# Attention and ternary feed-forward on one core: input rows of the second batch entry fetched and normalised one step earlier, in five buffers instead of three, and two start-up transposes in other PSUM buffers

## The chip, the core and the metric

The kernel runs on one core of a Trainium2 chip. The metric is device time in microseconds (us), the median of several runs. The profile is one execution of its own, with a time of its own. Engines are named as the profile names them: PE (matmul), PEld (its weight loads), DVE, ACT, POOL, and SP, whose queue issues the DMAs.

## The reference, cut to what matters

All data are fp32. Two batch entries of 1024 tokens and 512 features go through attention with 16 heads of 128 and then through a feed-forward layer whose three weights are rounded to -1, 0 or 1 times a scale.

```python
def attn(x):                                   # x: (2, 1024, 512)
    q, k, v = (einsum('bsd,hed->bhse', x, W) for W in (W_Q, W_K, W_V))
    scores = einsum('bhse,bhme->bhsm', q, k) / sqrt(128)
    scores = where(causal, -1e9, scores)
    z = einsum('bhsm,bhme->bhse', softmax(scores), v)
    return einsum('bhse,hde->bsd', z, W_O)

def ffn(x):                                    # hidden size 1365
    g = silu(x @ ternary(w1).T) * (x @ ternary(w3).T)
    return g @ ternary(w2).T

x = x + layernorm(attn(layernorm(x)))
out = x + layernorm(ffn(layernorm(x)))
```

## The kernel before

**Tiling.** A batch entry is 8 row tiles of 128 tokens. A head is worked in 8 steps, one for each row tile of queries; tile i needs scores against (i+1) x 128 keys. Two entries of 16 heads give 32 heads of 8 steps, and the loop at L813 to L894 walks them: head n is head n % 16 of entry n // 16. Every projection is done as three products of rounded parts, so weights and inputs are each held in three forms, "lead" (`a`), "low" (`l`) and "difference" (`d`).

**What one step does.** `scores` (L551) multiplies on PE into a PSUM tile `s_ps`, then DVE applies the mask (L561) and takes the row maximum (L565), ACT takes the exponential (L572), DVE the reciprocal of the row sums (L577), and ACT scales the row (L578) into `p_sb`. DVE turns the row in 32x32 squares (L604), SP writes it to DRAM (`hop`, L615) and reads it back turned (`pt`, L631), and PE multiplies it with v (L650). In between, PE does the projections of the next head (q and k: L471 and L478; v: L499) and the output product of a pair of heads (L519, added into `acc` by DVE at L530 and L533). Weights come in by L423; their lead form is made by ACT (L439), their low form by POOL (L440), their difference form by DVE (L446).

**Input blocks.** The rows x of an entry are normalised (L388 on ACT, or L123 on DVE), transposed by PE in four pieces into one PSUM tile (L403, `block_unit`), and read from there into the three forms `xb`: lead on ACT (L407), low on DVE (L408), difference on POOL, in two start-up tiles on DVE (L409). For the first entry this happens at the start, from `acc`. For the second entry row tile t is transposed at step 117 + t, counted over all heads, so in heads 14 and 15: `block_load` (L380) fetches the rows into a buffer `xt` of the pool "x", `normal_unit` normalises them there. The same pool serves the row sums of the feed-forward weights (L148 and L154, heads 0 to 9), the input statistics of the second entry (L354 and L109) and the residual rows (L279).

**Order.** `side[...]` is a list of units of work per step; the units are recorded behind named marks of the step. A scheduler then puts the instructions of each engine into one fixed order, which it chooses by its own estimate of when operands are there and buffers are free. Each engine runs its list strictly in that order, and so does the SP queue; an instruction that waits holds up all behind it on its engine. A tile of a pool gets a buffer that is free or is the first to come free. Pool "ps_m" holds four PSUM buffers (tag `mm`: projections, transposes, products with v), pool "ps_s" two larger ones (scores, and the transposes of the first entry).

**The start.** PE first runs 20 transposes of the identity (`busy(20)`, L703), then the transposes of row tiles 0 and 1, `busy(8)`, those of tiles 2 and 3, `busy(3)`, and then the q and k projections of head 0.

```python
side[block_at - 3 + t].append(lambda t=t: block_load(1, t))     # L752, block_at = 117
side[block_at - 2 + t].append(lambda t=t: normal_unit(1, t))    # L753
```

Of the kernel before, what the change touches and what calls it, by code (L numbers as in the profile page):

```python
# [35 lines left out]
def sandwich_kernel(  # L36
# [85 lines left out]
    def normalise(dst, src, mv, r, t):  # L122
        return nc.vector.tensor_scalar(  # L123
            dst, src, mv[:, t, 0:1], r[:, t : t + 1], ALU.subtract, ALU.mult
        )
# [212 lines left out]
    with ExitStack() as att:  # L338
# [4 lines left out]
        vpool = att.enter_context(tc.tile_pool(name="v", bufs=2))  # L343
        zpool = att.enter_context(tc.tile_pool(name="z", bufs=ZB))
        qpool = att.enter_context(tc.tile_pool(name="q", bufs=2))
        xpool = att.enter_context(tc.tile_pool(name="x", bufs=3))
        ps_s = att.enter_context(tc.tile_pool(name="ps_s", bufs=2, space=PSUM))


# [7 lines left out]
        def stats_units(t):  # L357
            held = {}

            def load():  # L360
                held["x"] = stats_load(1, t)

            return load, lambda: row_stats(mv_in[1][:, t, :], held["x"])
# [14 lines left out]
        def block_load(b, t):  # L378
            normal[b, t] = xt = xpool.tile([P, D], FP, name="xt")
            nc.sync.dma_start(xt, x[b, ts(t, P), :])  # L380

        def normal_unit(b, t):
            if b == 0:
                normal[b, t] = acc[:, t, :]
            xt = normal[b, t]
            if b == 0 and t % 2 == 1:
                return normalise(xt, xt, mv_in[b], r_in[b], t)
            return nc.scalar.activation(  # L388
                xt, xt, AF.Identity, scale=r_in[b][:, t : t + 1],
                bias=shifts[b][:, t : t + 1],  # L390
            )

        def block_unit(b, t):
            k, tl = divmod(t, QT)
            if tl == 0:
                xs[b, k] = [xblocks.tile([P, NC, TB], FR, name="xb") for _ in range(3)]
            xt = normal[b, t]
            if b == 0:
                ps = ps_s.tile([P, NC, P], FP, name="tr", tag="s_ps")
            else:  # L400
                ps = ps_m.tile([P, NC, P], FP, name="tr", tag="mm")
            for c in range(NC):
                newest[0] = nc.tensor.transpose(ps[:, c, :], xt[:, ts(c, P)], ident)  # L403
            lead, low, diff = (form[:, :, ts(tl, P)] for form in xs[b, k])
            eng = nc.vector if b == 0 and tl >= QT // 2 else nc.gpsimd
            return (
                nc.scalar.mul(lead, ps, LEAD / T12),  # L407
                nc.vector.scalar_tensor_tensor(low, lead, -T12, ps, ALU.mult, ALU.add),  # L408
                eng.tensor_tensor(diff, lead, low, ALU.subtract),  # L409
            )  # L410
# [19 lines left out]
        def lead_and_low(kind, n, part, first=False):  # L430

            if (kind, n) not in weights:
                weights[kind, n] = [form(kind, "a"), form(kind, "l")]
            lead, low = (w[:, part] for w in weights[kind, n][:2])
            raw = wraw[kind, n][:, part]
            if first:
                nc.vector.tensor_scalar(lead, raw, LEAD, None, ALU.mult)
            else:
                nc.scalar.mul(lead, raw, LEAD)  # L439
            nc.gpsimd.tensor_tensor(low, raw, lead, ALU.subtract)  # L440
# [241 lines left out]
        @contextmanager  # L682
        def past(*instructions):
            with ExitStack() as order:
                for i in instructions:
                    order.enter_context(tc.issue_after(i.ins))
                yield
# [10 lines left out]
        def busy(times):  # L698
            with ExitStack() as order:
                if newest[0] is not None:  # L700
                    order.enter_context(past(newest[0]))
                for _ in range(times):
                    newest[0] = nc.tensor.transpose(idle, ident, ident)  # L703
# [4 lines left out]
        with past(*done):  # L708
            for kind in range(2):
                lead_and_low(kind, 0, EVERY, first=True)  # L710
            blocks = []
            for t in range(QT):
                blocks.append(block_unit(0, t))
                if t % 2 == 1:
                    busy((8, 3)[t // 2])
        lead, low, diff = blocks[-1]
        with past(diff):
            for kind in range(2):
# [12 lines left out]
        side = [[] for _ in range(N * NT)]  # L731
        at = 0

        def two_steps_each(pairs, at):
            for first, then in pairs:
                side[at].append(first)
                side[at + 2].append(then)
                at += 2
            return at

        for k in range(3):
            pairs, total, last = mean_abs_units(k, xpool)
            at = two_steps_each(pairs, at)
            side[at + 1].append(total)
            side[at + 3].append(last)
        at = two_steps_each([stats_units(t) for t in range(NT)], at)
        side[at + 1].append(lambda: std_unit(1, 0, NT))

        block_at = 2 * (NP - 1) * NT + 5
        assert at + 1 < block_at - 3  # L750
        for t in range(NT):
            side[block_at - 3 + t].append(lambda t=t: block_load(1, t))  # L752
            side[block_at - 2 + t].append(lambda t=t: normal_unit(1, t))  # L753
        at += (1 - at) % 4 + 4
        for stages in ternary_steps(qpool):
            for later, stage in zip((0, 2, 3, 4), stages):
# [46 lines left out]
        for t in range(QT, NT):  # L803
            block_unit(0, t)
# [8 lines left out]
        for n in range(N):  # L813
            g, j = divmod(n, 2)
            b, pr = divmod(g, NP)
# [23 lines left out]
            for t in range(NT):  # L839
                if divmod(block_at + t, NT)[0] == n:  # L840
                    put([(block_at + t) % NT], [lambda t=t: block_unit(1, t)])
# [5 lines left out]
            for i in range(NT):  # L847
# [23 lines left out]
                with behind("max", "half", "exp", of=idx + 1):  # L871
# [4 lines left out]
                    at = g + 1 - j  # L876
# [26 lines left out]
    with ExitStack() as ffn:  # L903
# [4 lines left out]
        xpool = ffn.enter_context(tc.tile_pool(name="xf", bufs=3))  # L908
# [208 lines left out]
```

## Time and profile before

| | us |
|---|---|
| median of 3 runs | 1512.0 |
| the runs | 1510.33 to 1512.47 |
| time of the profiled execution | 1511.27 |
| its span, first to last instruction | 1509.5 |
| PE busy | 1475.6 |
| DVE busy | 1080.6 |
| ACT busy | 792.7 |
| POOL busy | 404.3 |
| mean granted TensorE clock | 0.997 |

Some 1.8 us of the profiled execution's time lie outside its span. All times below are in us from the start of the span. A group "x4" in a timeline is four instructions of one line that follow each other; "[1.27 <-ACT xt L388]" behind a row says that the engine sat idle for 1.27 us before it, until that instruction had ended. SPq rows are the issue of a DMA, not its transfer. Matmuls are pipelined: a row's duration holds the end of its own result, and the next one starts before that.

### The profile page before, as it was taken

To read this page: it belongs to the slowest core of one execution; us is meant where nothing else is said; L and a number is where in the kernel's file an instruction comes from. 1 tells how busy PE (TensorE), PEld (TensorE's weight loads), DVE (VectorE), ACT (ScalarE), POOL (GpSimd) and SP (SyncE) were. 2 spreads that over 40 slices of the span, in tenths; PEclk is the share of its full clock that TensorE was granted. 3 is DMA by queue.
4 is the path that set the end of the run, shared out by engine and by line. 5 is a ranking of instruction groups with operands and counts; after the bars stand their busy time and mean duration, and the time that the engine had idled before them with its cause. 6 is when DMAs were issued, how large, how long until landed. Compare 5 with 4: busy or idle time off the path is not lost.

```text
span 1509.5 us, 21335 instructions
## 1 busy us (share of the span) xinstructions
PE 1475.6 (98%) x7061; PEld 1184.9 (78%) x7061; DVE 1080.6 (72%) x2123; ACT 792.7 (53%) x1566; POOL 404.3 (27%) x472
## 2 busy tenths in 40 slices
PE   8999999999999999999999999999999999999997
PEld 6778888887878787777778787878787877888885
DVE  7767686878786878787777777777777776664444
ACT  4656555555555555666664555555555464444332
POOL 3222222222223333434433333333322110210010
PEclk9999999999999999999999999999999999999999
DMA  3666767676666675758866666666665677530200
GB/s 123 194 194 186 195 184 200 185 202 184 201 191 172 181 206 183 205 166 249 238 200 190 195 192 196 195 195 189 179 179 166 181 216 228 176 102 19 91 28 29
DMA packets 179894, 263.57 MB, mean 175 GB/s; under 512 B 19188, under 2 KB 120564, under 8 KB 175688
## 3 DMA queue, kind: packets, MB, share of 16 engines
q1 hardware_dynamic: 179784, 262.20, 59.5%
q8 instruction: 57, 0.93, 0.3%
q14 instruction: 53, 0.43, 0.1%
HBM read 160.43 MB, written 101.71 MB: 174 GB/s over the span
## 4 chain that ended last, share of the span: by engine, by line
PE 66%; issue 10%; DVE 9%; DMA 7%; ACT 5%; POOL 2%; SPq 1%; DVEq 0%; POOLq 0%; ACTq 0%
PE mm L650 11%; PE mm L471 10%; PE mm L318 10%; PE s_ps L556 10%; PE mm L499 8%; PE mm L519 6%; PE yp L933 5%; PE mm L478 5%; DVE nm L565 3%; DMA hop<-blocks 2%; ACT p_sb L572 2%; DMA wqk<-wk 2%; ACT p_sb L578 1%; POOL kl L440 1%; DVE blocks L604 1%
## 5 line engine op out<-in xcount | busy, mean ns | idle before, releaser
L572 ACT ACTIVATE p_sb<-s_ps,nm 128x128 f32<-128x128 f32 (+7 forms) x256 | 190.0, 742 | 367.3 <-DVE nm L565 360.8
L556 PE MATMUL s_ps<-k,q 128*128 128x512 f32 (+3 forms) x768 | 289.7, 486 | 0.7 <-ACT p_sb L572 0.7
L650 PE MATMUL mm<-pt,v_sb 128*128 128x256 f32 (+1 forms) x1280 | 271.7, 359 | 11.3 <-ACT q L454 3.7
L650 PEld LDWEIGHTS mm<-pt,v_sb 128*128 128x128 f32 x1280 | 238.1, 190 | 48.8 <-ACT q L454 6.2
L578 ACT ACTIVATE p_sb<-p_sb,ri 128x128 f32<-128x128 f32 (+7 forms) x256 | 197.7, 773 | 33.0 <-DVE ri L577 30.5
L565 DVE TENSOR_REDUCE nm<-s_ps 128x1 f32<-128x128 f32 (+7 forms) x256 | 193.7, 757 | 7.1
L604 DVE STREAM_TRANSPOSE blocks<-p_sb 128x128 f32<-128x128 f32 (+7 forms) x256 | 197.1, 770 | 1.2 <-ACT p_sb L578 0.9
L556 PEld LDWEIGHTS s_ps<-k,q 128*128 128x128 f32 x768 | 132.3, 190 | 69.4 <-issue 61.4
L670 POOL TENSOR_TENSOR zd<-za,zl 128x256 fp32r<-128x256 f32 x128 | 94.7, 739 | 328.0 <-DVE zl L667 319.7
L561 DVE TENSOR_TENSOR s_ps<-s_ps,causal 128x128 f32<-128x128 f32 x256 | 75.4, 295 | 136.1 <-PE s_ps L556 135.6
L499 PE MATMUL mm<-va,xb 128*128 128x256 f32 x512 | 158.5, 310 | 0.0
L499 PE MATMUL mm<-vd,xb 128*128 128x256 f32 x512 | 144.9, 283 | 0.9 <-POOL xb L409 0.9
L499 PE MATMUL mm<-vl,xb 128*128 128x256 f32 x512 | 144.6, 282 | 0.0
L471 PE MATMUL mm<-xb,qa 128*128 128x512 f32 x256 | 119.6, 467 | 1.0 <-ACT xb L407 1.0
L471 PE MATMUL mm<-xb,ka 128*128 128x512 f32 x256 | 112.3, 439 | 0.0
L499 PEld LDWEIGHTS mm<-vl,xb 128*128 128x128 f32 x512 | 97.7, 191 | 7.1 <-issue 4.1
L499 PEld LDWEIGHTS mm<-va,xb 128*128 128x128 f32 x512 | 97.7, 191 | 7.1 <-issue 3.9
L471 PE MATMUL mm<-xb,ql 128*128 128x512 f32 x256 | 101.7, 397 | 0.0
L471 PE MATMUL mm<-xb,kl 128*128 128x512 f32 x256 | 100.7, 393 | 0.1
L499 PEld LDWEIGHTS mm<-vd,xb 128*128 128x128 f32 x512 | 97.7, 191 | 1.1 <-POOL xb L409 1.1
L601 POOL MEMSET blocks<- 128x128 f32 x128 | 26.2, 205 | 263.1 <-DMA hop<-blocks 185.2
L533 DVE TENSOR_TENSOR acc<-acc,mm 128x512 f32<-128x512 f32 x128 | 86.1, 683 | 12.7 <-ACT acc L528 5.4
(162 smaller groups left out, 2777.3 us busy)
## 6 DMA issues: line engine op xcount, KB each, us to landing
hop<-blocks SPq DMA_DIRECT2D x32, 1024.0 KB, 4.5
pt<-hop SPq DMA_DIRECT2D x128, 256.0 KB, 6.2
hop<-blocks SPq DMA_DIRECT2D x32, 768.0 KB, 3.3
pt<-hop SPq DMA_DIRECT2D x128, 192.0 KB, 3.8
hop<-blocks SPq DMA_DIRECT2D x32, 512.0 KB, 3.2
pt<-hop SPq DMA_DIRECT2D x128, 128.0 KB, 3.2
wqk<-wq SPq DMA_DIRECT2D x32, 256.0 KB, 5.2
wqk<-wk SPq DMA_DIRECT2D x32, 256.0 KB, 6.6
```

Source lines behind the costliest of these rows:

```text
L318: newest[0] = nc.tensor.matmul(ps[:fl, :], lhsT=t[:, c, :], rhs=bl[k][:, c, :], start=(c == 0 and k == 0), stop=(c == NC - 1 and k == 1),)
L471: newest[0] = nc.tensor.matmul(main, lhsT=forms[f][0][:, c, :], rhs=forms[f][1][:, c, :], start=(c == 0 and f == 0), stop=(c == NC - 1 and ...
L499: newest[0] = nc.tensor.matmul((main, main, diff)[f][:, ts(t, 2 * P)], lhsT=forms[f][0][:, c, token], rhs=forms[f][1][:, c, :], start=(t = ...
L519: newest[0] = nc.tensor.matmul((main, main, diff)[f], lhsT=zs[g, t // QT, j][f][:, ts(t % QT, P)], rhs=weights[3, g][f][:, 2 * j : 2 * j + ...
L533: nc.vector.tensor_tensor(dst, dst, diff, ALU.subtract)
L556: newest[0] = nc.tensor.matmul(s_ps[:, ds(k0, kl)], lhsT=proj[n, 0, i // QT][:, ts(i % QT, P)], rhs=proj[n, 1, k0 // TB][:, :kl], start=Tr ...
L565: top = nc.vector.tensor_reduce(nm, s_ps[:, :L], axis=AX.X, op=ALU.max, negate=True)
L572: e = nc.scalar.activation(p_sb[:, :L], s_ps[:, :L], AF.Exp, bias=nm, accum_out=rs)
L578: nc.scalar.mul(p_sb[:, :L], p_sb[:, :L], ri)
L604: turned = nc.vector.transpose(b[:, :, 0 : i + 1, il, :].rearrange("p to t r -> p t to r"), p_sb[:, :L].rearrange("p (b r) -> p b r", r=32),)
L650: newest[0] = nc.tensor.matmul(dst, lhsT=proj[g, 2][:, kt, ts(j, P)], rhs=rhs, start=(kt == 0), stop=(kt == 2 * m + 1),)
L670: nc.gpsimd.tensor_tensor(diff, lead, low, ALU.subtract)
```

## The change

Four edits:

- Pool "x" has five buffers instead of three.
- In `block_unit` of the first entry, row tiles 2 and 3 take a PSUM buffer of "ps_m" instead of one of "ps_s".
- The two `busy` groups have 7 and 8 transposes instead of 8 and 3.
- The loads and the normalisations of the second entry's row tiles are recorded one step earlier: load at step 113 + t, normalisation at 114 + t, transposes as before at 117 + t.

```diff
-        xpool = att.enter_context(tc.tile_pool(name="x", bufs=3))
+        xpool = att.enter_context(tc.tile_pool(name="x", bufs=5))
...
-            if b == 0:
+            if b == 0 and t not in (2, 3):
                 ps = ps_s.tile([P, NC, P], FP, name="tr", tag="s_ps")
             else:
                 ps = ps_m.tile([P, NC, P], FP, name="tr", tag="mm")
...
-                    busy((8, 3)[t // 2])
+                    busy((7, 8)[t // 2])
...
-        assert at + 1 < block_at - 3
+        assert at + 1 < block_at - 4
         for t in range(NT):
-            side[block_at - 3 + t].append(lambda t=t: block_load(1, t))
-            side[block_at - 2 + t].append(lambda t=t: normal_unit(1, t))
+            side[block_at - 4 + t].append(lambda t=t: block_load(1, t))
+            side[block_at - 3 + t].append(lambda t=t: normal_unit(1, t))
```

As the scheduler orders anew, more moves than the lines say. Between the two built programs:

- PE: the same order, but for the two `busy` groups.
- ACT: in nine heads (2 to 10) the lead form of a v or output weight (L439) stands ahead of the scaling of row tile 4 (L578, 128x640) instead of behind it. In heads 14 and 15 the eight normalisations L388 stand elsewhere (below, in the prediction).
- DVE: three swaps of neighbours in heads 14 and 15, the first of which puts the second q of head 15 (L458) ahead of L530 and L533.
- POOL: a few swaps in head 15.
- SP: in nine heads of the first entry the 512 KB weight load L423 (wv or wo) stands ahead of the four reads of the widest `pt` instead of behind them and the next hop, and the rows for L154 come three after one another behind the narrowest hop. The first load L380 is no longer issued four heads ahead.

## The prediction

> **What bounds the kernel now.** I read the page first, then busy times by stretch, then who PE waited for, then the timelines of the two places that the change touches: the start and heads 14 to 15.
>
> ```profile
> PE 1475.6 (98%) x7061; PEld 1184.9 (78%) x7061; DVE 1080.6 (72%) x2123; ACT 792.7 (53%) x1566; POOL 404.3 (27%) x472
> ```
>
> ```profile
> 13.00:16.50 3.50, 3.50 (x9) 2.50 (x10) 3.50 (x4) 0.90 (x2) 3.50 (x3) 0.51 0.27 109
> ...
> 192.00:268.00 76.00, 76.00 (x371) 61.21 (x370) 58.43 (x118) 39.82 (x84) 18.13 (x25) 1.00 0.67 192
> ...
> 590.00:610.00 20.00, 18.55 (x109) 16.03 (x110) 14.58 (x31) 11.53 (x26) 9.76 (x9) 1.00 0.76 206
> 610.00:630.00 20.00, 18.42 (x89) 13.79 (x88) 14.07 (x25) 14.95 (x29) 11.42 (x11) 1.00 0.63 186
> ```
>
> The columns after the length are busy us of PE, PEld, DVE, ACT, POOL, then the granted clock. Two heads in the steady part keep PE busy for 76.00 of 76.00 us: there nothing that another engine gains counts. PE has holes at the start, and in heads 14 and 15, and at 13.00 to 16.50 its clock is half. PE's waits from 550 to 720:
>
> ```profile
> PE mm L650 <- DVE acc L530: 3.2, 2, 1.7
> PE mm L478 <- ACT q L454: 1.6, 1, 1.6
> PE tr L403 <- ACT xt L388: 1.6, 2, 1.3
> PE mm L499 <- POOL xb L409: 0.9, 1, 0.9
> ```
>
> The third row is what an earlier normalisation can take away: 1.6 us. Its place, on PE and then on ACT:
>
> ```profile
> 612.38 0.66 PE L403 MATMUL tr<-ident,xt 128*128 128x128 f32 x4 [1.27 <-ACT xt L388]
> 612.87 1.25 PE L556 MATMUL s_ps<-k,q 128*128 128x512 f32 x4
> 614.42 0.65 PE L403 MATMUL tr<-ident,xt 128*128 128x128 f32 x4 [0.31 <-ACT xt L388]
> ```
>
> ```profile
> 613.07 0.60 ACT L407 ACTIVATE xb<-tr 128x512 fp32r<-128x512 f32 x1 [0.23 <-PE tr L403]
> 613.56 1.51 ACT L388 ACTIVATE xt<-xt,shift,r_in 128x512 f32<-128x512 f32 x2
> 615.11 0.60 ACT L407 ACTIVATE xb<-tr 128x512 fp32r<-128x512 f32 x1
> 615.61 0.79 ACT L572 ACTIVATE p_sb<-s_ps,nm 128x640 f32<-128x640 f32 x1
> ...
> 616.89 0.82 ACT L578 ACTIVATE p_sb<-p_sb,ri 128x640 f32<-128x640 f32 x1
> ```
>
> The transposes at 612.38 are tile t=4's, those at 614.42 tile t=5's, with the scores of 640 keys between them. Tile 5's normalisation ran ahead of the exponential of those scores (613.56 against 615.61). This order matters below.
>
> **The change part by part.**
>
> *Start.* The transposes of tiles 2 and 3 no longer wait for DVE to leave the "ps_s" buffers.
>
> ```profile
> 10.97 1.25 PE L403 MATMUL tr<-ident,acc 128*128 128x128 f32 x8 [1.83 <-DVE xb L408]
> 12.06 0.49 PE L703 MATMUL idle<-ident 128*128 128x128 f32 x3
> 12.91 0.67 PE L471 MATMUL mm<-xb,qa 128*128 128x512 f32 x1 [0.36 <-ACT xb L407]
> ```
>
> They need only their normalised rows, ready at 9.71 (ACT L388 8.90 + 0.81), so they start near 9.78, 1.2 us sooner. ACT ends its first two leads at 10.68, so the next two run 10.65 to 11.75 instead of to 12.86; DVE's lows follow its first two (to 11.51) and end at 12.7 instead of 13.59. DVE is then one queue: differences 2.37, qd 1.77, kd 1.77, vd 1.28, row statistics. It stays dense, slowed by POOL as before, so it is some 0.8 us early, and so is the normalisation of tile 4, for which PE sits idle until 24.63. POOL isn't moved (its kl ends at 12.37), which is why I take 0.8 and not 0.9; bounds 0.5 and 1.0. The eight `busy` transposes end near 11.6, before the last lead: they delay nothing. They fill PE's hole and should keep the clock up: the half clock at 13.00 to 16.50 followed a stretch in which PE worked 1.67 of 3.5 us (9.50 to 13.00). But that clock is worth nothing by itself: at full clock PE would be done with the leads and lows near 16.0 and wait for qd (about 16.7). [...] Sum: -0.8.
>
> *Heads 2 to 10.* ACT's lead form (0.61) goes ahead of the scaling of row 4. It drops into ACT's 0.39 us wait for the reciprocal; the scaled row, ended at 156.37 in one head, was read by DVE at 158.71: 0.2 late against 2.3 spare, 0. The SP queue: a 512 KB load now stands ahead of the widest pt reads, where a 256 KB one stood. These reads were issued from 294.86 to 296.6 and land 5.6 us after issue in that stretch, 302.2; PE used them at 304.20. Another 256 KB at that stretch's 193 GB/s are 1.3 us: covered, with 0.7 left. In the heads with wv the load first waits for PE's L499 (to 331.3), so the reads go out 1.8 us late, but PE needs them only at 342.1. Cost 0; if the cover fails, up to 1 us in five or six heads.
>
> *Heads 14 and 15.* In the new ACT order tile 0's L388 goes between the exponential of the 768-key row of head 14 and its scaling: 0.7 there, q's L454 falls behind both, and DVE, which waits for it, is 1.5 us late at 581 (q's L454 ends at 580.86 instead of 579.33). PE is touched by 0.45 us, and then gets it back: its 1.65 us wait at 590.54 was for L530, behind DVE's queue; the buffer now comes from q's L454 (590.15), and PE goes on at 590.21, 0.33 early. The 0.92 us wait for POOL's difference of tile 3 stays, as POOL makes ql first: ql to 607.90, difference to 609.17, so PE is 0.43 early. Tile 4's L388 now stands ahead of the exponential of the 384-key row, done by 603.3, so its transposes start without a wait at 610.51: 1.87 early.
>
> Now what is late next. Tile 5's load comes behind the pt reads of the SP queue (it goes out near 602.3), the scheduler took it for late, and in the new ACT order tile 5's L388 stands *behind* the exponential and the scaling of the 640-key row. PE's order is unchanged: tile 4, scores of 640 keys, tile 5. So tile 5's transposes wait for the whole softmax of scores that PE has just made, and all of PE waits behind them. From 610.51, with durations of the rows before: tile 4's transposes to 611.16; ACT v 0.58, scaling 0.7, lead of tile 4 0.6, to 612.43; DVE low 0.69 to 613.16, mask to 613.36, maximum 0.82 to 614.22; exponential with its read-out to 615.20; DVE's turn 0.70 and reciprocal, to 615.41; scaling 0.82 to 616.29; L388 0.80 to 617.00; PE at 617.06. The scores ended at 612.24: PE idles 4.8 us, and tile 5 starts 2.6 us later than before (614.42). From there all that follows in the PE queue is 2.6 late. The chain after the scores has 4.1 us even if DVE were free at once: bounds +1.9 and +3.1. Sum: +2.6.
>
> *The clock.* A 4.8 us hole is longer than any in this profile. At the start the clock fell to half for 3.4 us after a stretch with PE 48% busy and no hole over 1.83. [...]
>
> Sum: -0.8 + 0 + 2.6 + 1.7 = +3.5. Against the profiled execution's own 1511.27 (span 1509.5 and 1.8 around it) that is 1514.8; this execution lies 0.7 below the median of the runs, so 1515.5 against 1512.0.
>
> **The rivals.**
>
> *The hole without the clock.* PE stays at full clock after it, or the holes at 670 to 710 (L530 and L454, 3.1 us together) shrink since ACT and DVE have caught up meanwhile. [...] Against: those holes are made by short local chains which shift along. -0.8 + 2.6 = +1.8: 1513.8.
>
> *Faster: the wait just goes.* If tile 5's L388 ended before the scores do, at 612.2, the hole wouldn't form: PE keeps -1.87 at tile 4 and gains the 0.31 at tile 5, with 0.3 more of slack behind it, -2.5 together, and -0.8 at the start: 1508.7. For it: loads are early enough (issue 602.3, landing 4.6 later). Against: ACT keeps its list.
>
> *Slower in the steady heads.* The pt reads behind 512 KB miss PE's 304.20: past 2 us of delay each of five or six heads loses up to 1. 1515.5 + 5 = 1520.5. Against: 1.3 of 2.0.
>
> *The start doesn't gain*, because POOL slows DVE more when they overlap longer: +0.8 on the main case, inside its range.
>
> **How the numbers follow.** What a measurement of this kernel can tell from no change is about 0.2%, 3.0 us: the borders are 1509.0 and 1515.0. Main case 0.68, itself 1514.0 to 1517.0, so 0.49 beyond the border and 0.19 within; no clock loss 0.15, all within; steady heads 0.09, slower; the wait just goes 0.08, faster. Slower 0.58, same 0.34, faster 0.08. The likeliest is 1515.5; the range 1511.5 to 1518.5 leaves out the faster case and the bulk of the steady one.
>
> **What would show it.** A PE row L403 near 616 (all shifted by -0.8) with some 4.8 us idle before it, ended by ACT L388, and on ACT L572 and L578 of 128x640 before it; the wait of 1.27 at tile 4 gone; a clock of 0.5 for 3.4 us or more behind the hole, and none at 13 to 16; tile 4 of the first entry transposed near 23.8; in 192 to 268 PE busy throughout. I am wrong if tile 5's L388 runs before that exponential, if the hole is under 3 us, or if PE waits for pt in heads 2 to 10.

## The result and the profile after

| | before | after |
|---|---|---|
| median, first comparison | 1511.65 us | 1518.12 us (4 runs, 1517.05 to 1520.61), ratio 1.0046, 95% interval 1.0029 to 1.0063 |
| second comparison | 1511.95 us | 1516.47 us (5 runs), ratio 1.0032, 1.0019 to 1.0045 |
| third comparison | 1512.47 us | 1517.01 us (6 runs), ratio 1.0031, 1.0020 to 1.0043 |
| profiled execution | 1511.27 us, span 1509.5 | 1517.95 us, span 1516.2 |

The changed kernel is slower by 0.3 to 0.5%. The forecast was 1515.5; all 15 runs of it together have their median at 1517.2. To see where the time went, each matmul of the scores (L556) on PE was paired with the same one in the profile of before; how much later it starts is called the shift. It is -0.1 us at the end of head 1, +2.9 at the end of head 13, +0.9 just ahead of the hole that the prediction expected, +7.0 behind it, and +6.7 at the end of the attention. So nothing came from the start, 3.0 from the steady heads, and 3.8 from head 14 to the end of the attention (4.1 in heads 14 and 15, of which 0.3 comes back in head 29).

The page's line of busy times, then the busy times of the same four stretches (columns: length, busy us of PE, PEld, DVE, ACT, POOL, granted clock, DMA share, GB/s):

```profile
PE 1478.3 (98%) x7065; PEld 1186.8 (78%) x7065; DVE 1077.9 (71%) x2123; ACT 791.2 (52%) x1566; POOL 404.4 (27%) x472
```

```profile
13.00:16.50 3.50, 2.95 (x13) 2.08 (x12) 3.50 (x3) 1.11 (x2) 3.50 (x3) 1.00 0.70 270
192.00:268.00 76.00, 75.65 (x369) 60.78 (x368) 57.54 (x115) 39.41 (x85) 17.94 (x24) 1.00 0.67 192
590.00:610.00 20.00, 18.92 (x107) 15.94 (x106) 16.21 (x34) 12.71 (x27) 7.84 (x9) 1.00 0.81 220
610.00:630.00 20.00, 14.59 (x72) 11.74 (x71) 10.68 (x21) 10.55 (x20) 8.99 (x10) 0.91 0.71 209
```

The last line is the loss at the switch of entries: PE busy 14.59 us where it was 18.42, and the mean clock below 1. The second shows a loss that wasn't forecast: 0.35 us of idle PE in two heads that had none. Who PE waited for, from 550 to 720 (us in total, times, longest):

```profile
PE tr L403 <- ACT xt L388: 4.7, 1, 4.7
PE mm L478 <- ACT q L454: 1.6, 1, 1.6
PE mm L650 <- DVE acc L530: 1.5, 1, 1.5
PE mm L650 <- ACT q L454: 1.1, 1, 1.1
PE mm L499 <- POOL xb L409: 0.7, 1, 0.7
```

Two waits for L388, 1.6 us together, have become one of 4.7. One of the two waits for L530 became a shorter one for L454. The place, in the timelines of PE and of ACT (start, length, and in brackets the idle time before and what ended it):

```profile
613.37 0.60 PE L403 MATMUL tr<-ident,xt 128*128 128x128 f32 x4
613.81 1.25 PE L556 MATMUL s_ps<-k,q 128*128 128x512 f32 x4
619.73 0.66 PE L403 MATMUL tr<-ident,xt 128*128 128x128 f32 x4 [4.67 <-ACT xt L388]
620.22 5.09 PE L650 MATMUL mm<-pt,v_sb 128*128 128x256 f32 x16
```

```profile
617.03 0.79 ACT L572 ACTIVATE p_sb<-s_ps,nm 128x640 f32<-128x640 f32 x1 [1.88 <-DVE nm L565]
...
618.14 0.83 ACT L578 ACTIVATE p_sb<-p_sb,ri 128x640 f32<-128x640 f32 x1 [0.23 <-DVE ri L577]
618.88 0.80 ACT L388 ACTIVATE xt<-xt,shift,r_in 128x512 f32<-128x512 f32 x1
```

Tile 4's transposes (613.37) run without a wait; tile 5's (619.73) wait for the whole softmax of the scores that PE made just before. L650 x16 behind the hole takes 5.09 us at half clock (0.50 from 620.30 to 623.70). In the steady heads, from 40 to 550:

```profile
PE mm L650 <- DMA pt<-hop: 2.7, 3, 1.3
PE mm L650 <- DVE qd L446: 1.1, 1, 1.1
```

One wait of the first row is that of head 0's widest product (at 76.6), which before has as well; the other two, and the second row, are new (that row names qd, but its product at 115.74 follows pt reads that came late). At the start, the timelines of DVE and of POOL:

```profile
12.29 3.25 DVE L409 TENSOR_TENSOR xb<-xb 128x512 fp32r<-128x512 f32 x2
15.46 1.76 DVE L446 SCALAR_TENSOR_TENSOR qd<-ql,qa 128x512 fp32r<-128x512 f32 x1
```

```profile
12.01 2.98 POOL L409 TENSOR_TENSOR xb<-xb 128x512 fp32r<-128x512 f32 x2
14.95 3.41 POOL L440 TENSOR_TENSOR vl<-wvo,va 128x512 fp32r<-128x512 f32 x2
```

The same rows in the profile of before:

```profile
13.51 2.37 DVE L409 TENSOR_TENSOR xb<-xb 128x512 fp32r<-128x512 f32 x2
15.80 1.77 DVE L446 SCALAR_TENSOR_TENSOR qd<-ql,qa 128x512 fp32r<-128x512 f32 x1
```

```profile
12.32 3.01 POOL L409 TENSOR_TENSOR xb<-xb 128x512 fp32r<-128x512 f32 x2
15.29 3.42 POOL L440 TENSOR_TENSOR vl<-wvo,va 128x512 fp32r<-128x512 f32 x2
```

DVE begins its two differences sooner, 12.29 for 13.51, and takes 3.25 us over them for 2.37: qd begins at 15.46 for 15.80, and that third of a microsecond is how much earlier this execution had begun with its first transposes (6.83 for 7.18).

Taken one instruction at a time, the trace shows DVE and POOL working in turn here. In the changed kernel DVE's first difference begins at 12.29, inside POOL's first (12.01 to 13.28), and ends at 13.83. Its second begins inside POOL's second (to 14.98) and ends at 15.54. Then qd begins inside POOL's first vl (to 16.67) and ends at 17.22. Each ends some 0.55 us behind the POOL instruction that it met. In before, DVE's first difference begins at 13.51, just as POOL's first (12.32 to 13.60) is ending, and takes 0.68; the second difference and qd again end 0.55 behind POOL's second difference (15.33) and first vl (17.02). So the end of qd hangs on POOL's list, which the change does not move. In before's whole profile all 17 of DVE's L446 that begin inside a POOL TENSOR_TENSOR (L440 or L670) end 0.55 to 0.65 us behind it.

### The profile page after: what moved, and what is told of

It reads as the page before. It is cut to its first block, busy times and chain, and to the rows that moved or that the text cites. A ratio compares the mean times of both kernels' runs of the same rounds, so it can differ in the third digit from the quotient of the medians.

```text
span 1516.2 us, 21342 instructions
## 1 busy us (share of the span) xinstructions
PE 1478.3 (98%) x7065; PEld 1186.8 (78%) x7065; DVE 1077.9 (71%) x2123; ACT 791.2 (52%) x1566; POOL 404.4 (27%) x472
## 4 chain that ended last, share of the span: by engine, by line
PE 59%; DMA 11%; issue 10%; DVE 10%; ACT 6%; POOL 3%; SPq 1%; DVEq 0%; POOLq 0%; ACTq 0%
PE mm L318 10%; PE mm L650 10%; PE mm L471 9%; PE s_ps L556 9%; PE mm L499 6%; PE mm L519 5%; DMA hop<-blocks 5%; PE yp L933 5%; PE mm L478 4%; DVE nm L565 3%; ACT p_sb L572 3%; DMA pt<-hop 2%; DMA wqk<-wk 1%; DVE blocks L604 1%; ACT p_sb L578 1%
## 5 line engine op out<-in xcount | busy, mean ns | idle before, releaser
L556 PE MATMUL s_ps<-k,q 128*128 128x512 f32 (+3 forms) x768 | 289.7, 486 | 0.7 <-ACT p_sb L572 0.7
L650 PE MATMUL mm<-pt,v_sb 128*128 128x256 f32 (+1 forms) x1280 | 273.6, 361 | 13.4 <-DMA pt<-hop 5.0
L650 PEld LDWEIGHTS mm<-pt,v_sb 128*128 128x128 f32 x1280 | 239.2, 191 | 51.7 <-ACT q L454 7.5
L578 ACT ACTIVATE p_sb<-p_sb,ri 128x128 f32<-128x128 f32 (+7 forms) x256 | 197.7, 773 | 28.6 <-DVE ri L577 26.2
L556 PEld LDWEIGHTS s_ps<-k,q 128*128 128x128 f32 x768 | 132.3, 190 | 69.3 <-issue 61.4
L670 POOL TENSOR_TENSOR zd<-za,zl 128x256 fp32r<-128x256 f32 x128 | 94.6, 739 | 332.5 <-DVE zl L667 324.0
L533 DVE TENSOR_TENSOR acc<-acc,mm 128x512 f32<-128x512 f32 x128 | 86.0, 682 | 11.5 <-ACT acc L528 5.3
```

The source lines that it names most:

```text
L533: nc.vector.tensor_tensor(dst, dst, diff, ALU.subtract)
L556: newest[0] = nc.tensor.matmul(s_ps[:, ds(k0, kl)], lhsT=proj[n, 0, i // QT][:, ts(i % QT, P)], rhs=proj[n, 1, k0 // TB][:, :kl], start=Tr ...
L578: nc.scalar.mul(p_sb[:, :L], p_sb[:, :L], ri)
L650: newest[0] = nc.tensor.matmul(dst, lhsT=proj[g, 2][:, kt, ts(j, P)], rhs=rhs, start=(kt == 0), stop=(kt == 2 * m + 1),)
L670: nc.gpsimd.tensor_tensor(diff, lead, low, ALU.subtract)
```

## The experiments

**1. Each part alone.** `start_only` has the PSUM edit and the busy groups; `bufs5_only` the five buffers; `step_only` the loads and normalisations a step earlier, with three buffers.

```diff
 start_only:  -            if b == 0:
              +            if b == 0 and t not in (2, 3):
              -                    busy((8, 3)[t // 2])
              +                    busy((7, 8)[t // 2])
 bufs5_only:  -  tc.tile_pool(name="x", bufs=3)
              +  tc.tile_pool(name="x", bufs=5)
 step_only:   -  side[block_at - 3 + t] ... block_load;  side[block_at - 2 + t] ... normal_unit
              +  side[block_at - 4 + t] ... block_load;  side[block_at - 3 + t] ... normal_unit
```

> Only the PSUM edit and the two busy groups; pool and loads as before. Theory: DVE's two differences L409 now run beside POOL's and take 3.25 instead of 2.37 us, so qd, kd and vd come no earlier and the half clock only moves from 13 to 19.5 us: the scores of head 1 on stand within 0.2 us of before, time 1512 (1511.3 to 1512.5). Rival, the prediction's own step: tile 4 is transposed 0.8 us earlier, 1511.2.

> Only the pool x with five buffers. Theory: the loss in heads 2 to 10 belongs to the buffers alone, since they let the scheduler put the 512 KB weight load ahead of the widest pt reads; PE waits for pt in heads 2, 5 and 9, together 3.0 us, and nothing happens in heads 14 and 15 beyond that: 1515 (1514 to 1516). Rival: the waits in those heads come from the phase that the start gives them (0.1 to 0.3 us earlier), not from the order of loads: no wait for pt, 1512.

> Only load and normalisation one step earlier, three buffers. Theory: nothing in heads 2 to 10; in heads 14 and 15 tile 5's L388 stands behind the exponential and scaling of the 640-key row, so PE has a hole of 4.7 us before tile 5's transposes and half clock for 3.4 us behind it; net 3.5 to 4 us: 1515.8 (1515 to 1516.5). Rival: with three buffers the loads wait for buffers anyway and tile 4's 1.3 us wait stays, so the switch costs over 5 us: 1517.5.

Measured, beside before at 1511.68: `start_only` 1511.16 (ratio 0.9998, 0.9989 to 1.0007), `bufs5_only` 1511.23 (0.9997, 0.9988 to 1.0005), `step_only` 1516.47 (1.0026, 1.0015 to 1.0037).

The start is worth nothing: the shift is +0.1 from head 1 on. `bufs5_only` went against my theory: its shift grows by 0.4 us where the first profile of the changed kernel lost 3.0. The rival has the time right, but not the reason: the order of loads does take away the cover (experiment 2). `step_only` holds most of the loss (4.8 us between the medians). It has the hole at the same place, and a half clock of 6.83 us that began within the hole, so that L650 x16 suffers more than in the changed kernel (PE's timeline of `step_only`):

```profile
617.88 1.12 PE L403 MATMUL tr<-ident,xt 128*128 128x128 f32 x4 [4.68 <-ACT xt L388]
618.79 5.26 PE L650 MATMUL mm<-pt,v_sb 128*128 128x256 f32 x16
```

Five buffers are thus not needed for the hole: recording the step earlier is enough to put L388 of tile 5 behind the exponential.

**2. The weight load behind the pt reads again.** `after_load_back` is the changed kernel with one constraint.

```diff
-                    if j == 0 and g + 1 < G and i == 1 + (n == 0):
-                        load_raw(2, g + 1)
-                    if j == 1 and i == 1:
-                        load_raw(3, g)
+                    vo = [(2, g + 1)] if j == 0 and g + 1 < G and i == 1 + (n == 0) else []
+                    for kind, at in vo + ([(3, g)] if j == 1 and i == 1 else []):
+                        with past(*brought[-2:-1]):
+                            load_raw(kind, at)
```

> The changed kernel with one constraint: the weight load of v or the output stands behind the widest pt reads again, as before; the row loads of the wider pool stay early. Theory: the delay of the pt reads is that load's, so the 3.0 us of heads 2 to 10 go: 1515.2 (1514.3 to 1516), with the hole in head 15 unchanged. Rival: the row loads that the five buffers let in ahead are what the reads share the DMA engines with, so the waits for pt stay and it is 1518.

Measured 1516.09 (1.0029, 1.0018 to 1.0040). What the constraint undoes is seen in the timeline, in the rows of the SP queue and of PE's product; first the changed kernel, then before, whose order the constraint brings back (the products go on past these views, which end at 231):

```profile
219.00 0.33 SPq L423 DMA_DIRECT2D wvo<-wo  x1
...
220.25 1.75 SPq L631 DMA_DIRECT2D pt<-hop  x4
...
230.03 1.32 PE L650 MATMUL mm<-pt,v_sb 128*128 128x256 f32 x5 [0.35 <-DMA pt<-hop]
```

```profile
219.04 1.88 SPq L631 DMA_DIRECT2D pt<-hop  x4
...
223.12 0.57 SPq L423 DMA_DIRECT2D wvo<-wo  x1
...
228.32 2.97 PE L650 MATMUL mm<-pt,v_sb 128*128 128x256 f32 x13
```

Before, the reads go out 9.3 us ahead of the product; after, 9.8, yet behind 512 KB. For each of the nine heads concerned, the cover is the time from the last recorded landing of the four reads to PE's first product; 0.1 means that PE stood waiting. Over the nine heads, and what the shift grew by in them:

| profile | weight load | least cover | median | longest read | shift grew by |
|---|---|---|---|---|---|
| before | behind | 0.6 us | 4.2 | 8.7 us | - |
| `start_only` | behind | 1.6 | 3.7 | 8.1 | 0 |
| `step_only` | behind | 1.7 | 3.9 | 8.1 | 0 |
| `after_load_back` | behind | 0.9 | 4.3 | 8.3 | 0 |
| `bufs5_only` | ahead | 0.1 | 1.3 | 9.4 | 0.4 |
| changed kernel, first profile | ahead | 0.1 | 1.2 | 10.4 | 3.0 |

In most of these heads the landing of one to three of the four reads isn't recorded, so the true cover can be smaller: PE waited at 115.74 in the changed kernel although 1.3 was recorded there. The load takes 2.4 to 3.1 us of the median recorded cover. Whether a read was then late went with how long it took in that execution (the longest 9.4 us in `bufs5_only`, 10.4 in the changed kernel).

**3. The changed kernel again, beside the constrained one.**

> The changed kernel itself once more. With five buffers alone the reads of the widest pt came 0.1 to 2.2 us before PE needs them, and none was late by more than 0.2, while in the first profile of the changed kernel three were late, 3.0 us together. Theory now: the order of loads takes the cover away, and whether a read is late is decided anew in each execution by how long it takes (9.7 us and over is late), so the mean loss is below that profile's 3.0: median 1516.5 to 1517.5, and in the new profile waits for pt in other heads or none. Rival: the loss is built in, the same three heads wait again, 1518.1 or more.

> The changed kernel for a third time, beside the next one. Theory: with the weight load ahead of the pt reads an execution loses 0.5 to 3 us in heads 1 to 9, more in one than in the next: median 1517.2 (1516.4 to 1518.2), 1 us or more above the kernel with the load put back. Rival: in the mean the order of loads costs nothing, as five buffers alone cost nothing in 12 executions: both 1516.2.

> The changed kernel with the weight load behind the widest pt reads, again, beside the changed kernel itself. Theory: 1516.2 (1515.6 to 1516.8), 1 us or more below the changed kernel, with no late pt read in heads 2 to 10. Rival: the same as the changed kernel within 0.4 us.

Measured: `after_again` 1516.47, `after_third` 1517.01, `load_back_again` 1516.40. The cover is the same as in the first profile (least 0.1, median 1.3), but the longest read took 9.5 us in both, not 10.4. The shift grew by 0.8 and 0.5: by 0.5 in both at the product near 230, whose cover before was the smallest of all (0.6), and in `after_again` by another 0.4 at the product near 115, where the first profile lost 1.3. The third late read of the first profile, near 383, didn't come again. All runs of the two kernels together: the changed one has a mean of 1517.4 over 15 runs (standard error 0.3), the constrained one 1516.4 over 13 (0.2). That makes 1.0 with an error of 0.4. The six profiles with the load ahead (these, and those of experiments 4 and 5) grew by 0.4, 3.0, 0.8, 0.5, 0.5 and 0.8. Against this stands that five buffers alone cost nothing in 12 runs, and that in the one comparison that ran both kernels the means are only 0.4 apart, where 1 us or more was expected. The mechanism is shown; its mean cost lies somewhere from nothing to 1.8 us (two standard errors), and more exactly it stays open.

`load_back_again` showed what a late read can cost beyond its wait. In its profile the product of head 0, late in every profile, came later still; PE's timeline, and the busy times of the stretch behind it:

```profile
77.40 5.17 PE L650 MATMUL mm<-pt,v_sb 128*128 128x256 f32 x16 [2.16 <-DMA pt<-hop]
```

```profile
78.60:82.00 3.40, 3.40 (x10) 2.64 (x9) 0.00 (x0) 0.86 (x2) 1.27 (x1) 0.50 0.71 215
```

The second is a stretch of 3.4 us with a clock of 0.50, and the shift went from -0.4 to +2.4 there: 1.1 more wait than the 1.04 of before, and 1.7 for the product, which took 5.17 us for 3.48. The waits of 0.9 to 1.75 us at this place in the other profiles drew no half clock.

**4. The hole taken away: tile 5 normalised first.** `after_norm_first` is the changed kernel with one exponential held back.

```diff
+            normal[t] = nc.scalar.activation(xt, xt, AF.Identity, ...)      # in normal_unit
...
+            held = [normal[5]] if (n, i) == (2 * NP - 1, 4) else []         # in scores
+            with past(*held): e = nc.scalar.activation(p_sb[:, :L], ...)
```

> The changed kernel with the exponential of the 640-key row of head 15 held until tile 5 is normalised, so that ACT makes L388 of tile 5 first. Tile 5's rows landed at 614.2 in the first profile, so L388 ends near 615.1, when the scores of 640 keys end. Theory: the hole of 4.7 us shrinks to 0.5 or less, there is no half clock behind it, and 5.5 to 6.5 us go: 1511.5 (1510.5 to 1512.5). Rival: tile 5's lead form, now behind two more normalisations whose rows land at 616.9, keeps its PSUM buffer and PE stops 2 to 3 us later on: 1514 or more.

Measured 1510.67 (0.9993, 0.9986 to 0.9999), 5.8 below the changed kernel of the same comparison. The timelines of this kernel, PE and then ACT:

```profile
614.06 0.66 PE L403 MATMUL tr<-ident,xt 128*128 128x128 f32 x4 [0.85 <-ACT xt L388]
614.55 3.41 PE L650 MATMUL mm<-pt,v_sb 128*128 128x256 f32 x16
```

```profile
613.20 0.81 ACT L388 ACTIVATE xt<-xt,shift,r_in 128x512 f32<-128x512 f32 x1
615.19 0.79 ACT L572 ACTIVATE p_sb<-s_ps,nm 128x640 f32<-128x640 f32 x1 [1.18 <-DVE nm L565]
```

The exponential lost nothing by standing behind: it still waits for DVE's maximum. The hole is 0.85 us, a little more than the 0.5 expected, and L650 x16 takes 3.41 again. From the start of head 15 to behind the hole the shift falls by 1.2 us; in the first profile of the changed kernel it rose by 4.3. One place in ACT's list is the whole difference, and the rival's next wait didn't come.

**5. The hole kept, the clock kept up.** `after_fill` puts 36 transposes of the identity on PE ahead of tile 5's, into the PSUM buffer that those then overwrite.

```diff
+            for c in [None] * (36 * ((b, t) == (1, 5))) + list(range(NC)):
+                # None: nc.tensor.transpose(ps[:, 0, :], ident, ident)
```

> The changed kernel with 36 transposes of the identity on PE in the hole, ahead of tile 5's, into the PSUM buffer that tile 5's then overwrite: 4.3 us at 0.12 each, inside the hole of 4.7. Only the clock can change. Theory: the half clock behind the hole is the hole's doing, and work of this kind keeps it away: tile 5's product L650 x16 takes 3.4 us as before instead of 5.1, and 1.7 to 2.3 us go, 1515 (1514.3 to 1516.2). Rival: [...] the clock falls for another reason: L650 x16 takes 5.1 again, 1517.

PE's timeline of this kernel, and the busy times of the 10 us around it:

```profile
612.64 4.09 PE L403 MATMUL tr<-ident 128*128 128x128 f32 x36
617.49 0.66 PE L403 MATMUL tr<-ident,xt 128*128 128x128 f32 x4 [0.75 <-ACT xt L388]
617.98 3.41 PE L650 MATMUL mm<-pt,v_sb 128*128 128x256 f32 x16
```

```profile
612.00:622.00 10.00, 9.25 (x62) 8.02 (x61) 4.32 (x8) 6.93 (x13) 3.99 (x5) 1.00 0.66 225
```

With identity transposes in the hole the clock stays at 1.00 and L650 x16 takes 3.41; in the six profiles with the hole left open a half clock came and it took 5.09 to 5.88. So the half clock went with the hole. The runs agree: their mean granted clock is 0.9972 over the 10 of this kernel and 0.9956 over the 15 of the changed one. From the start of head 15 to behind the hole the shift grows by 2.6 us; in the three profiles of the changed kernel it grew by 4.3, 5.0 and 5.8. So the hole itself is 2.6, which is what the prediction had, and the clock adds 1.7 to 3.2. The time says less: 1516.11 (1.0026, 1.0017 to 1.0035), only 0.4 below `after_again`. In this profile the shift grew by another 1.7 us behind head 15, where that of `after_again` stayed as it was; 0.7 of it are three waits for pt, the rest wasn't traced.

A half clock came here without the hole too. `start_dve` (experiment 7) has the order of before in heads 14 and 15, where no wait of PE from 600 to 616 is over 1.27 us, and in its profile the clock fell to half at 615.69 for 3.41 us; its shift grew by 1.8 there. PE's timeline:

```profile
612.77 0.39 PE L499 MATMUL mm<-vd,xb 128*128 128x256 f32 x1 [0.92 <-POOL xb L409]
615.50 0.97 PE L403 MATMUL tr<-ident,xt 128*128 128x128 f32 x4 [1.27 <-ACT xt L388]
616.27 2.34 PE L556 MATMUL s_ps<-k,q 128*128 128x512 f32 x4
```

The profiles of before, `start_only` and `bufs5_only`, with the same order there, had none. With the hole it came in six of six.

**6. A version that is faster.** `both_back` has five buffers, the earlier step, and the constraints of 2 and 4; the start is that of before.

> Five buffers and the earlier step, the start as before, the weight load of v or the output behind the widest pt reads, and tile 5 normalised ahead of the exponential of the 640-key row. Theory: nothing is lost in heads 2 to 10, the hole and the half clock are gone, and tile 4's transposes come without a wait (some 1.9 us as seen at that place in all traces with the earlier step), so it is 1 to 2 us faster than before: 1510.3 (1509.3 to 1511.3). Rival: the gain at tile 4 is given back at the next wait of heads 16 to 18, 1511.7.

Measured 1510.15 (0.9990, 0.9982 to 0.9998): faster by 0.1%. Its shift grows by nothing in heads 2 to 10, falls by 1.2 from the start of head 15 to behind the place of the hole, and stays down: half of the 2.5 us that the rival "the wait just goes" had for this place.

**7. Why the start gained nothing.** `start_dve` has the start edits, and the differences of tiles 0 and 1 on DVE instead of POOL. `all_three` is the changed kernel with this and with the constraints of 2 and 4.

```diff
-            eng = nc.vector if b == 0 and tl >= QT // 2 else nc.gpsimd
+            eng = nc.vector if b == 0 and (t < QT or tl >= QT // 2) else nc.gpsimd
```

> The PSUM and busy edits alone, and the differences L409 of tiles 0 and 1 on DVE instead of POOL. Theory: DVE and POOL slow each other while both run; with the two POOL differences (2.99 us) gone, POOL is done with vl near 15.3 instead of 18.2, so qd and kd take some 0.7 us each instead of 1.76 and, although DVE has two differences more, vd ends 1 us earlier than the 19.9 of the start edits alone; the scores of head 1 on stand 0.7 to 1.5 us before those: 1510.2 (1509.5 to 1511.2). Rival: DVE's own length sets the start; two more differences (1.3 us and more beside POOL) make it later: 1512.3.

> The changed kernel with all three causes put right: weight load behind the widest pt reads, tile 5 normalised ahead of the exponential of the 640-key row, and the differences L409 of the first entry's tiles 0 and 1 on DVE. Theory: the gains add, -1.3 in heads 14 and 15 and -1 at the start: 1509.5 (1508.7 to 1510.5), faster than before and than the kernel with two put right. Rival: what the start gains is taken back by the 1.0 to 1.5 us wait for pt in head 1 (at 76.6), which every trace so far has: 1510.3.

DVE's timeline of `start_dve`:

```profile
11.09 3.16 DVE L409 TENSOR_TENSOR xb<-xb 128x512 fp32r<-128x512 f32 x2
14.17 1.27 DVE L408 SCALAR_TENSOR_TENSOR xb<-xb,tr 128x512 fp32r<-128x512 f32 x2
15.37 1.28 DVE L409 TENSOR_TENSOR xb<-xb 128x512 fp32r<-128x512 f32 x2
16.57 0.68 DVE L446 SCALAR_TENSOR_TENSOR qd<-ql,qa 128x512 fp32r<-128x512 f32 x1
```

The first half of the theory holds. In this kernel POOL works from 9.40 to 15.38. Two differences that overlap it take 3.16 us and two that don't take 1.28; qd takes 0.68 for 1.76; and vd ends at 19.06 for the 19.97 of `start_only`. The two slow differences end 0.55 us behind POOL's kl (12.03) and first vl (13.70), so again in turn. POOL's took longer too: in before the first vl, beside qd, 1.73 us at 15.29, and kl 1.28 at 11.09. DVE's L408, with one of its two inputs in PSUM, didn't: 1.27 for two at 14.17, beside POOL, and in before 0.67 to 0.69 each for the six beside a POOL instruction, 0.65 to 0.69 for the ten others.

The second half failed. The lows of tiles 2 and 3 now stand behind two differences, and PE waits for them; PE's timeline of `start_dve`, and the busy times of the stretch with the low clock:

```profile
15.59 0.76 PE L471 MATMUL mm<-xb,ql 128*128 128x512 f32 x1 [3.49 <-DVE xb L408]
```

```profile
14.95:21.75 6.80, 6.16 (x15) 4.83 (x16) 5.31 (x9) 0.60 (x1) 0.43 (x1) 0.50 0.00 0
```

The clock is half for 6.8 us, from 14.95 in this hole on, the products for v begin at 23.57 instead of 20.41 in the profile of before, and the shift is +1.8 in head 0. Times: `start_dve` 1511.98 (1.0002, 0.9992 to 1.0012), `all_three` 1511.39 (0.9993, 0.9985 to 1.0002), beside before at 1512.47. Both were expected to be faster; neither beats `both_back`. The profile of `all_three` had the half clock too, from 16.45 for 3.41 us, and its shift is +1.6 at the end of head 1. A version with DVE free of POOL and the lows first was not tried.

## Why the prediction was right or wrong

The first profile moved by 6.7 us where 3.5 was forecast. Two terms account for it: the steady heads, put at 0, lost 3.0 in it, and the start, put at -0.8, gained nothing. The switch was 0.5 below its forecast in this profile and 0.5 above it in the mean of six.

- **Heads 14 and 15, the hole: right.** Forecast 4.8 us, measured 4.67, with the named order on ACT (exponential, scaling, L388), tile 4 without a wait (the shift falls by 1.8 there; forecast 1.87), and 2.6 net by experiment 5.
- **The clock: half behind the hole, as forecast; too small in the mean.** The forecast's 1.7 was the author's estimate: half of a half clock of 3.4 us, as the start of before has one (0.50 from 13.08 to 16.49). The first profile had 3.41 us at half clock after the hole, so 1.7. The five other profiles with the hole had a half clock of 6.83 us that began inside it, and 4.4 to 5.9 us of it fell on work: 2.2 to 3.0. The term that was mis-sized is the length: 3.4 us were taken, and twice as much came in five of six. The mean of all six is 2.4. For the whole switch 4.3 was forecast; the six profiles give 3.8 to 5.7, mean 4.8. In the 3.41 us ahead of each of the 16 half clocks that these profiles show amid the work, PE was busy for 0 to 1.75 us (1.75 ahead of 13.08 in before, 1.74 and 0.56 ahead of 19.54 and 620.29 in the changed kernel). That every such stretch draws one is not shown.
- **The start, -0.8: wrong.** The step that failed is "DVE is then one queue ... It stays dense, slowed by POOL as before, so it is some 0.8 us early". DVE was not slowed by a fixed amount; it took turns with POOL. Its two differences began 1.2 us sooner and went from 2.37 to 3.25 us, and qd ended 0.35 us earlier (17.22 for 17.57), which is by how much POOL's first vl was earlier in this execution (16.67 for 17.02). The prediction saw that POOL isn't moved, and took 0.1 off for it. It had the miss as a rival, but as one in which POOL slows DVE "when they overlap longer"; in before POOL works beside both differences too, and only the first one's place in the turns made it fast (0.68 and 1.76). That the `busy` group keeps the clock up was half right: the clock at 13.00 to 16.50 is 1.00, and a half clock came at 19.54 instead, behind PE's waits for qd and kd (1.42 and 0.44). Of the eight profiles with this start three show it, at 19.1 to 19.5, and five show none. The statement that this clock is worth nothing by itself held: `bufs5_only`, with before's start, had no half clock there at all, and its scores at the end of head 0 are 0.5 us early, which is no more than its first transposes are (6.70 for 7.18).
- **Heads 2 to 10, 0: wrong in the margin.** The step that failed is "covered, with 0.7 left". It was worked out from one head, the read used at 304.20, with a cover of 2.0 us from a median landing; the last recorded landing leaves 1.6. The cost of the load, put at 1.3, was 2.4 to 3.1 in the median cover. Before's profile has another, used at 228.32, with 0.6; there 1.3 us could not fit, and every profile with the load ahead lost something. In the first profile two more reads were late, and 3.0 us were lost together. The "slower in the steady heads" rival had the mechanism, but at 5 us it was too large: single heads lose, in some executions.
- **The sum.** -0.8, 0, 2.6 and 1.7 were forecast; the first profile shows 0, 3.0 and 3.8 for start, steady heads and switch. The repeated profiles put the middle term nearer 0.5 to 1. With 0, 0.5 to 1 and 4.8 the sum is 5.3 to 5.8; the 15 runs have a mean 5.5 above that of all 99 runs of before (1512.0).
- **"The wait just goes"** could not have come as written. Tile 5's load was issued at 605.5, not 602.3, and its rows landed at 614.2, behind the end of the scores that the prediction named (612.2). Where the order was put right (experiment 4), the rows landed at 612.24, L388 began at 613.20, behind tile 4's lead form on ACT, and PE still waited 0.85 us.

## What to carry to other kernels

A step recorded earlier for the benefit of one tile can move another tile's producer behind a long chain on its engine (here tile 5's L388 on ACT, at 4.67 us of idle PE): list, for every tile, what stands ahead of its producer after the change, and pin that one order if it is wrong. Check a cover at every place that repeats, and take the smallest, not the one that was looked at first. DVE began its differences 1.2 us sooner here and gained nothing by it, as its instructions still took turns with those of POOL, whose list hadn't moved: look also at which instructions of other engines run beside those that come sooner.

## What the runs showed of the hardware that was not expected

- Amid the work, a half clock lasted 3.413 us (at 13.08 in before, at 19.54 and 620.29 in the changed kernel) or 6.83 (in the five other profiles with the hole), and it began inside a hole or behind it: at the same hole of 4.7 us it began at 620.29 (hole ended 619.73) in one execution of the changed kernel and at 615.42 (hole ended 617.38) in `after_again`. What it added at this hole differed by 1.3 us between executions (1.7 to 3.0).
- A single wait of 2.16 us in a stretch of otherwise dense work was followed by 3.4 us of half clock; waits of 0.9 to 1.75 us at the same place were not. Two waits of 0.92 and 1.27 us, 2.7 us apart, were (`start_dve`, 615.69).
- DVE's L409 and L446, both inputs in SBUF, took turns with POOL's TENSOR_TENSOR, whole instruction by whole instruction: one of 0.68 us alone took up to 1.8 (1.77 at 15.80 in before), and ended some 0.55 us behind the POOL instruction that it met.
- The same four reads of 256 KB behind the same load (those used near 383) took from 8.0 to 10.4 us from the first issue to the last recorded landing in six profiles.
